# A chain of modulated convolutions on one core: 18 products for W, shared products of R between them, S's sums on VectorE

## The chip, the cores and the metric

The kernel runs on one core of a Trainium2 chip. TensorE (PE in the profile; PEld is its weight load) multiplies matrices into PSUM; VectorE (DVE), ScalarE (ACT) and GpSimd (POOL) work on tiles, and SyncE (SP) issues most DMAs. Each engine takes its own queue in order; semaphores tie the queues together. The metric is the device time of one execution in microseconds.

## The reference, cut to what matters

Four convolution layers of 64 channels and three taps (`same`, `upsample`, `same`, `downsample`) with weights that each of the 128 samples scales for itself, and the input added at the end:

```python
def _layer(x, style, w, b, mw, mb, typ):
    s = style @ mw.T + mb
    weight = SCALE * w * s[:, None, :, None]
    demod = lax.rsqrt(jnp.sum(weight * weight, axis=(2, 3)) + EPS)
    weight = weight * demod[:, :, None, None]
    if typ == 'same':
        out = jax.vmap(_conv_same)(x, weight) + b[None, :, None]
    elif typ == 'upsample':
        out = jax.vmap(_conv_up)(x, weight.transpose(0, 2, 1, 3)) + b[None, :, None]
        out = _blur(out, 2.0 * blur_k, (1, 1))
    elif typ == 'downsample':
        xb = _blur(x, blur_k, (2, 2))
        out = jax.vmap(_conv_down)(xb, weight) + b[None, :, None]
    return out
...
out = x
for i, typ in enumerate(TYPES):
    out = _layer(out, style, weights[i], biases[i], mod_w[i], mod_b[i], typ)
x = x + out
```

`x` is 128 x 64 x 1024 in float32. There is no nonlinearity between the layers.

## The kernel before, in words

Since everything is linear, the kernel folds the four layers of a sample into one filter of nine taps and applies that filter to the input once. Four samples make a quad; there are 32 quads (`NQ`), and the main loop's turn q (`turn_of`, q = 4 to 28; `early_turn` for 0 to 3, a written-out tail after 28) works on several quads at once: on q and n = q + 1 (applying the filter), on c = q + 2 (making W, the filter), and on s = q + 4 (the start of the chain of weights). The order in which each engine gets its instructions is the order in which the calls stand in the code (`manual_schedule`).

The chain of weights of one quad, each step products on TensorE in blocks of 64 columns (one block a tap) and an eviction by ScalarE that scales by the sample:

- `scale3` scales the last layer's taps (tile wd).
- `stage1_a` and `stage1_b` multiply by layer 2's taps into psS. ScalarE evicts four blocks to S (L360) behind stage1_a; behind stage1_b VectorE adds two more to them (L442), and GpSimd adds a third pair of blocks (L445).
- `stage2` multiplies S by the taps E of layer 1 with its blur, into psR. Three of its products are the same for two blocks each: `share` makes them a turn earlier from two sums of S's blocks (`share_sums`, VectorE, L462), in free columns (from NB + 4 on) of the two PSUM banks psA of quad q; `share_copy` (ScalarE, L490) copies each twice into psR, and `stage2_rest` adds the rest. ScalarE evicts to R.
- `stage3_b` and `stage3_a` multiply R by layer 0's taps to the nine taps W of the filter (L571), 12 and 7 products of 64 columns. GpSimd prepares two sums of R's blocks (`r_sums`, L588). stage3_b uses psA of quad n, four of its blocks are copied into psW by ScalarE, and stage3_a adds to those. ScalarE evicts all to Wf.
- `combine_a` and `combine_b` (VectorE) make from W the factors H of a fast form of the filter, and `residual` (L659) adds the input's share, a scaled identity, to the middle tap.

The filter is applied as five products of 340 columns (L753, `conv0` to `conv4`, each 12 matmuls in three groups) to transformed inputs T, which VectorE (`in_g01`, `in_g2`, `in04`, `in3`, L711) and GpSimd (`in1`, L726, `in2`, L731) make from the input X. psA of a quad collects conv3 (copied away by `copy_m3`), then conv1 (`sum1` on VectorE makes y1 from it), then conv2; `sum2` then makes Y from the copy and psA in two instructions, one a bank, and subtracts psA from y1 (L812); conv4 adds to Y in PSUM, conv0 to psA. `outputs(q, i)` evicts one of the three phases (psA, y1, Y) by ScalarE (L830) into the tile o and has SyncE store it.

So a turn has this order on TensorE: stage2(c), conv2(q), stage3_b(c), conv4(q), stage3_a(c), conv3(n), stage1_a(s), conv0(q), stage1_b(s), share(c + 1), conv1(n). In turns 10, 14, 15 and 19 (`SLOTS`) products for the signal's ends stand ahead of conv1. share runs in turns 5 to 27.

Of the kernel before, what the change touches and what calls it, by code (L numbers as in the profile page):

```python
# [54 lines left out]
C = 64  # L55
# [8 lines left out]
def kernel(  # L64
# [199 lines left out]
    def var_newton(bs, ls=slice(0, NL)):  # L264
# [5 lines left out]
    tA, tB, tBn, tC, t0, t3, td, tb = (  # L270
        const.tile([P, NQ, 2], F32, name=n) for n in ("tA", "tB", "tBn", "tC", "t0", "t3", "td", "tb")
# [94 lines left out]
    w2n = const.tile([P, 5, C], F32, name="w2n")  # L366

    def split_weights():
        nc_g.tensor_copy(w3x[:, :K], w3)
        nc_g.tensor_scalar_mul(w2n[:, :K], woi[2], -1.0)  # L370
        for t, src in ((w3x, w3), (w2n, woi[2])):
            nc_g.tensor_add(t[:, K:], src[:, : K - 1], src[:, 1:])
# [32 lines left out]
    EVEN = slice(0, K, 2)  # L405

    def stage1(q, pool=None, engs=(nc_a, nc_a), between=None):
# [3 lines left out]
        for k, (at, at1) in enumerate(((0, 3), (3, 1), (1, 4))):  # L411
            tap_matmul(ps, wd, at, 2, woi[2][:, k, :], EVEN, first=k == 0)
            tap_matmul(ps, wd, at1, 1, woi[2][:, k, :], slice(1, 2), last=k == K - 1)
# [3 lines left out]
        for r in range(2):  # L417
            scaled_copy(engs[r], flat(st[r][:, 1:6]), ps[r][:, : 5 * C], tB[:, q, r : r + 1])
# [3 lines left out]
    def stage1_a(q, ps=None):  # L422

        ps = ps or unit(ps_w, f"psS{q}")
        wd = chain[q]
        tap_matmul(ps, wd, 2, 2, w2n[:, 0, :], EVEN, first=True)
        tap_matmul(ps, wd, 3, 2, w2n[:, 2, :], EVEN)
        tap_matmul(ps, wd, 1, 1, w2n[:, 1, :], slice(1, 2))
        st, t = s_tiles(q)
        for r in range(2):  # L430
            scaled_copy(nc_a, flat(st[r][:, :4]), ps[r][:, C : 5 * C], tBn[:, q, r : r + 1])
        chain[q] = wd, ps, st, t

    def stage1_b(q):

        wd, ps, st, t = chain[q]
        tap_matmul(ps, wd, 2, 1, w2n[:, 3, :], slice(3, 4))
        tap_matmul(ps, wd, 4, 1, w2n[:, 4, :], slice(4, 5), last=True)
        for r in range(2):
            p1 = st[r][:, 0:1, :].to_broadcast([P, 2, C])  # L440
            sums = ps[r][:, 2 * C : 6 * C].rearrange("c (a b o) -> c a b o", a=2, b=2)[:, :, 0]
            nc_v.scalar_tensor_tensor(  # L442
                st[r][:, 4:6, :], sums, tB[:, q, r : r + 1], p1, op0=ALU.mult, op1=ALU.subtract
            )
        nc_g.tensor_add(t[:, :, 2], t[:, :, 2], t[:, :, 0])  # L445
# [7 lines left out]
    def tap_differences():  # L453
# [4 lines left out]
        nc_g.tensor_sub(Ed[:, 4:], E[:, 3:8:4], E[:, 5:6].to_broadcast([P, 2, C]))  # L458

    def share_sums(q):  # L460
        t = whole[q]
        nc_v.tensor_add(t[:, :, 6:8], t[:, :, 1:5:3], t[:, :, 2:6:3])  # L462
# [13 lines left out]
    def share(q, ps):  # L476
# [3 lines left out]
        chain_matmul(p12, E[:, 2], chain[q], slice(6, 7))  # L480
        chain_matmul(p34, E[:, 6], chain[q], slice(6, 7))
        chain_matmul(p34, E[:, 5], chain[q], slice(7, 8), True)
        shared_ps[q] = [b[:, at[0] : at[2]] for b in ps]

    def share_copy(q):

        ps = unit(ps_w, f"psR{q}")
        for r in range(2):
            src = shared_ps[q][r].rearrange("c (a o) -> c a o", a=2)
            nc_a.copy(  # L490
                ps[r][:, C : 5 * C].rearrange("c (a b o) -> c a b o", a=2, b=2),
# [4 lines left out]
    def stage2_rest(q):  # L496

        ps = shared_ps.pop(q)
        block = lambda i, n=1: [b[:, i * C : (i + n) * C] for b in ps]
        apart = [b[:, : 4 * C].rearrange("c (a b o) -> c a b o", a=2, b=2)[:, :, 0] for b in ps]  # L500
        plan = (
            (apart, E[:, 0], slice(1, 4, 2)),
            (block(1), Ed[:, 0], slice(2, 3)),
            (block(2), Ed[:, 1], slice(1, 2)),
            (block(3), E[:, 2], slice(3, 4)),
            (block(3), Ed[:, 2], slice(2, 3)),
            (block(4), Ed[:, 3], slice(1, 2)),
# [1129 lines left out]
```

## Time and profile before

| | |
|---|---|
| time, median of 3 runs | 480.93 us (480.69 to 480.96) |
| span of the profiled execution | 478.0 us |
| the profiled execution with what lies around its span, taken as in the runs | 480.9 us |
| TensorE's granted clock, mean | 0.997 |
| sum2's instructions (L662, Y from m and psA) | 64, 517 ns each |
| the first sum of W in combine and others of 384 elements (L662) | 0.55 to 0.57 us each |
| scaled copies psW from psA (L360) | 100, 269 ns each |
| evictions Wf from psW, 128 x 256 | 50, 470 ns each |
| R's sums on GpSimd (L588) | 24, 737 ns each |
| S's sums on GpSimd (L445) | 28, 790 ns each |

The span is the time from the first to the last instruction of one profiled execution; the run's time is longer by what lies around it, 2.9 us. An engine's busy time counts overlapping instructions once. A row of a timeline holds the start, the duration from the first start to the last end, engine, line, operation, output and inputs, shape and count; what stands in brackets is the engine's idle time ahead and what ended it. A product of TensorE appears as two records for each of its four quarters of the array, so eight records are one product.

### The profile page before, as it was taken

How to read it: one execution, taken by the hardware profiler on the slowest of the kernel's cores; microseconds unless marked ns; L12 is line 12 of the kernel's file. 1: busy time of each engine (PE TensorE's matmuls, PEld its weight loads, DVE VectorE, ACT ScalarE, POOL GpSimd, SP SyncE). 2: the span in 40 equal slices, each digit the busy share in tenths (PEclk: the TensorE clock that was granted, in tenths of full speed). 3: DMA queues.
4: the chain of work that ended last, by engine and by line, in shares of the span. 5: the costliest groups of instructions: out<-in, count | busy, mean ns of one | idle time of the engine just before them, and what ended most of it. 6: DMA issues, size and time to landing. Idle time of an engine off the chain costs nothing.

```text
span 478.0 us, 26721 instructions
## 1 busy us (share of the span) xinstructions
PE 469.6 (98%) x11928; PEld 346.4 (72%) x11928; DVE 417.5 (87%) x690; ACT 310.1 (65%) x708; POOL 163.5 (34%) x197
## 2 busy tenths in 40 slices
PE   8999999999999999999999999999999999999995
PEld 7877788777878876677776677766887777766652
DVE  5889998879889998899979899979989999999895
ACT  5565666667666676666667666667666768766352
POOL 3434032663335342243432233422434432333200
PEclk9999999999999999999999999999999999999998
DMA  5406365544445554345543455533455554445125
GB/s 175 158 28 200 114 195 192 150 139 144 139 150 157 173 173 127 122 151 160 171 149 120 131 170 152 173 127 126 145 169 162 162 154 146 152 146 170 61 91 191
DMA packets 50514, 70.70 MB, mean 148 GB/s; under 512 B 5664, under 2 KB 47328, under 8 KB 50400
## 3 DMA queue, kind: packets, MB, share of 16 engines
q1 hardware_dynamic: 49808, 68.32, 45.8%
q8 instruction: 93, 1.52, 1.5%
q10 hardware_dynamic: 592, 0.69, 0.5%
q14 instruction: 21, 0.17, 0.1%
HBM read 35.36 MB, written 33.62 MB: 144 GB/s over the span
## 4 chain that ended last, share of the span: by engine, by line
PE 95%; DVE 4%; issue 0%; ACT 0%; ACTq 0%; DVEq 0%
PE psA L753 45%; PE Y L753 11%; PE psR L467 9%; PE psA L571 7%; PE psW L571 7%; PE psS L389 6%; PE psR L533 4%; PE psA L467 2%; PE Y L994 2%; DVE H L662 1%; PE Y L180 1%; PE Y L336 1%; DVE G L662 0%; PE psM L204 0%; DVE o L832 0%
## 5 line engine op out<-in xcount | busy, mean ns | idle before, releaser
L753 PE MATMUL psA<-T,H 64*64 64x340 f32 x2304 | 187.3, 447 | 0.8 <-DVE y L662 0.7
L753 PEld LDWEIGHTS psA<-T,H 64*64 64x64 f32 x2304 | 89.9, 133 | 50.0 <-issue 3.1
L662 DVE SCALAR_TENSOR_TENSOR G<-X 128x1376 f32<-128x1376 f32 (+2 forms) x65 | 78.1, 1207 | 1.1 <-DMA X<-in_x 0.9
L726 POOL TENSOR_TENSOR T<-G 128x684 f32<-128x684 f32 x28 | 46.5, 1659 | 73.1 <-DVE G L662 73.1
L445 POOL TENSOR_TENSOR S<-S 128x128 f32<-128x128 f32 x28 | 22.1, 790 | 144.1 <-ACT S L360 136.8
L360 ACT ACTIVATE R<-psR,tC 128x448 f32<-128x448 f32 x63 | 36.5, 630 | 46.3 <-PE psR L467 26.7
L753 PE MATMUL psA<-T,Wf 64*64 64x340 f32 x768 | 63.9, 446 | 0.0
L753 PE MATMUL Y<-T,Wf 64*64 64x340 f32 x768 | 62.8, 451 | 0.1
L662 DVE SCALAR_TENSOR_TENSOR Y<-m,psA 128x340 f32<-128x340 f32 x64 | 33.1, 517 | 28.0 <-PE psA L753 26.6
L360 ACT ACTIVATE psW<-psA 128x128 f32<-128x128 f32 x100 | 19.3, 269 | 50.3 <-PE psA L571 46.2
L740 DVE TENSOR_TENSOR T<-G 128x1368 f32<-128x1368 f32 (+1 forms) x33 | 50.7, 1540 | 0.0
L360 ACT ACTIVATE Wf<-psW,t 128x256 f32<-128x256 f32 (+2 forms) x76 | 32.7, 479 | 26.5 <-PE psW L571 26.2
L711 DVE TENSOR_TENSOR T<-X 128x684 f32<-128x684 f32 x32 | 47.9, 1496 | 0.0
L467 PE MATMUL psR<-S,E 64*64 64x64 f32 (+1 forms) x1472 | 46.5, 238 | 0.0
L731 POOL TENSOR_TENSOR T<-G 128x684 f32<-128x684 f32 x28 | 46.5, 1660 | 0.0
L389 PEld LDWEIGHTS psS<-wd,w2n 64*64 64x64 f32 x1120 | 35.0, 133 | 13.3 <-ACT S L360 0.8
L467 PEld LDWEIGHTS psR<-S,E 64*64 64x64 f32 x1472 | 39.6, 134 | 5.2 <-ACT psR L490 0.2
L753 PEld LDWEIGHTS Y<-T,Wf 64*64 64x64 f32 x768 | 29.6, 132 | 18.0 <-DVE Y L662 0.7
L830 ACT ACTIVATE o<-psA,tb,td 128x340 f32<-128x340 f32 x63 | 37.0, 647 | 6.3 <-PE psA L753 6.3
L753 PEld LDWEIGHTS psA<-T,Wf 64*64 64x64 f32 x768 | 29.1, 133 | 15.1
L830 ACT ACTIVATE o<-Y,tb,td 128x340 f32<-128x340 f32 x63 | 36.6, 637 | 4.5 <-PE Y L753 2.7
L830 ACT ACTIVATE o<-y,tb,td 128x340 f32<-128x340 f32 x62 | 38.5, 679 | 0.6 <-DVE y L812 0.6
(165 smaller groups left out, 832.4 us busy)
## 6 DMA issues: line engine op xcount, KB each, us to landing
out<-o SPq DMA_DIRECT2D x167, 170.0 KB, 2.6
X<-in_x SPq DMA_DIRECT2D x150, 172.0 KB, 3.6
X<-in_x SPq DMA_DIRECT2D x14, 516.0 KB, 5.3
out<-o SPq DMA_DIRECT2D x6, 510.0 KB, 5.4
out<-o SPq DMA_DIRECT2D x2, 340.0 KB, 3.0
Xe<-in_x_ends SPq DMA_DIRECT2D x1, 512.0 KB, 6.7
out<-o ACTq DMA_DIRECT2D x3, 170.0 KB, 2.3
par<-in_params SPq DMA_DIRECT2D x2, 192.0 KB, 3.4
```

The lines of the kernel that those rows point to most:

```text
L360: nc_a.activation(dst, src, AF.Copy, scale=f)
L389: nc.tensor.matmul(ps[r][cols, at * C : (at + n) * C], weight[rows], wd[c if r == 0 else 1 - c][rows, taps], start=first, stop=last, skip_ ...
L445: nc_g.tensor_add(t[:, :, 2], t[:, :, 2], t[:, :, 0])
L467: nc.tensor.matmul(dst[r][cols], weight[rows], st[c if r == 0 else 1 - c][rows, slots, :], start=False, stop=last, skip_group_check=True,)
L571: nc.tensor.matmul(dst[r][cols], weight[rows], t[rows, c, slots, :], start=first, stop=last, skip_group_check=True,)
L662: nc_v.scalar_tensor_tensor(out, x, f, y, op0=ALU.mult, op1=op)
L711: nc_v.tensor_sub(t[:, pairs, 0, :NJ], plane(X, 3, pairs), plane(X, 1, pairs))
L726: eng.tensor_add(t[:, :, 0, :NJ], plane(g, 2), plane(g, 1))
L731: eng.tensor_sub(t[:, :, 1, :NJ], plane(g, 2), plane(g, 1))
L740: nc_v.tensor_sub(t[:, pairs, :, :NJ], both(a, PL), both(b, 1))
L753: nc.tensor.matmul(ps[s][cols, :NB], w, Ts[q, tag][rows, c, i, g : g + NB], start=(g == 0 and m == 3), stop=(g == K - 1), skip_group_check ...
L830: nc_a.activation(dst, src, AF.Identity, bias=add, scale=d3)
```

## The change

It regroups the products of W, moves three steps to other places in the turn, and hands two steps to other engines:

- stage3_b makes three sums' products from GpSimd's sums, now three blocks in two instructions, one a half of R; copies of three blocks go to six of psW. stage3_b and stage3_a hold 7 and 11 products of 64 columns. The six evictions of stage3_a scale by three tables (t0, t0b, t0c) instead of taps that are scaled ahead.
- S's signs change (w2n, tBn go, En comes), and its blocks lie in other slots. In the main loop VectorE makes the third sum of stage1_b; GpSimd's addition stays in the early turns.
- The residual's scaled identity x3 is made by ScalarE (`identity`) behind R's eviction; VectorE adds it in one instruction.
- sum2's two instructions become one where `wide` holds (the main loop but its first turn).
- share stands inside stage3_b, ahead of its last entry; share_sums at the end of the turn before; conv0's first group ahead of stage1_a; the outputs of Y behind S's eviction, those of y1 behind share_copy.

```diff
-    def stage1_b(q):
+    def stage1_b(q, eng=nc_v):
...
         for r in range(2):
-            p1 = st[r][:, 0:1, :].to_broadcast([P, 2, C])
-            sums = ps[r][:, 2 * C : 6 * C].rearrange("c (a b o) -> c a b o", a=2, b=2)[:, :, 0]
+            at = slice(3, 6, 1 if eng is nc_v else 2)
+            sums = blocks(ps, at)[r]
+            n = sums.shape[1]
+            p1 = st[r][:, 0:1, :].to_broadcast([P, n, C])
             nc_v.scalar_tensor_tensor(
-                st[r][:, 4:6, :], sums, tB[:, q, r : r + 1], p1, op0=ALU.mult, op1=ALU.subtract
+                st[r][:, at, :], sums, tB[:, q, r : r + 1], p1, op0=ALU.mult, op1=ALU.add
             )
-        nc_g.tensor_add(t[:, :, 2], t[:, :, 2], t[:, :, 0])
+        if eng is not nc_v:
+            eng.tensor_add(t[:, :, 4], t[:, :, 4], t[:, :, 0])
...
     def r_sums(q, eng):
         t = chain[q]
-        eng.tensor_add(t[:, :, 7:9], t[:, :, 2:6:3], t[:, :, 3:7:3])
+        for r in (slice(0, 2),) if eng is nc_v else PAIR:
+            eng.tensor_add(t[:, r, 7:10], t[:, r, 0:6:2], t[:, r, 1:7:2])
...
-    def stage3_b(q, ps):
+    def stage3_b(q, ps, between=None):
...
         plan = (
-            (slice(0, 3), w0s[2][:, 2, :], slice(0, 7, 3)),
-            (slice(0, 2), w0s[2][:, 1, :], slice(1, 5, 3)),
-            (slice(0, 2), w0s[2][:, 0, :], slice(2, 6, 3)),
-            (slice(3, 4), w0s[0][:, 0, :], slice(0, 1)),
-            (slice(4, 5), w0s[1][:, 0, :], slice(1, 2)),
-            (slice(4, 5), w0s[1][:, 1, :], slice(0, 1)),
-            (slice(5, 7), w0s[0][:, 1, :], slice(7, 9)),
+            (slice(3, 4), w0s[1][:, 2, :], slice(5, 6)),
+            (slice(3, 4), w0s[1][:, 1, :], slice(6, 7)),
+            (slice(4, 5), w0s[2][:, 2, :], slice(6, 7)),
+            (slice(0, 3), woi[0][:, 1, :], slice(7, 10)),
         )
         for i, (at, weight, slots) in enumerate(plan):
+            if between and i == len(plan) - 1:
+                between()
             same_row(blocks(ps, at), weight, t, slots, i == 0, i == len(plan) - 1)
         pw = shared_w[q] = unit(ps_w, f"psW{q}")
-        src = blocks(ps, slice(5, 7))
-        for i, f in enumerate((1.0, 1.0 / 3.0)):
-            for dst, v in zip(blocks(pw, slice(i, i + 3, 2)), src):
-                scaled_copy(nc_a, dst, v, f)
-        stage3_out(q, ps, 0, 5)
+        same_row(blocks(pw, slice(0, 1)), woi[0][:, 0, :], t, slice(0, 1))
+        for r in range(2):
+            src = ps[r][:, : K * C].rearrange("c (a o) -> c a o", o=C)
+            dst = pw[r][:, C : 7 * C].rearrange("c (a b o) -> c a b o", b=2, o=C)
+            nc_a.copy(dst, src[:, :, None, :].to_broadcast([P, K, 2, C]))
+        for r, src in enumerate(blocks(ps, slice(3, 5))):
+            scaled_copy(nc_a, Wq[q][0][:, 7:9, r], src, t0[:, q, r : r + 1])
...
     def stage3_a(q):
...
         plan = (
-            (slice(0, 3, 2), Wd[:, 0], slice(3, 7, 3)),
-            (slice(0, 3, 2), w0s[0][:, 2, :], slice(1, 5, 3)),
-            (slice(1, 4, 2), Wd[:, 1], slice(2, 6, 3)),
-            (slice(1, 2), w0s[1][:, 0, :], slice(4, 5)),
+            (slice(1, 6, 2), Wd[:, 0], slice(1, 6, 2)),
+            (slice(2, 7, 2), Wd[:, 1], slice(0, 5, 2)),
+            (slice(2, 7, 2), woi[0][:, 0, :], slice(2, 7, 2)),
+            (slice(3, 6, 2), woi[0][:, 2, :], slice(1, 4, 2)),
         )
...
-    def sum2(q, steps=(0, 1)):
+    def sum2(q, steps=(0, 1), wide=True):
         if 0 in steps:
             m3 = m3c.pop(q)
-            for s, a in enumerate(banks(q)):
-                sum_of(Y[:, s, :NB], m3[:, s], 3.0, a[:, :NB])
+            whole = parts(q) if wide else [(s, a[:, :NB]) for s, a in enumerate(banks(q))]
+            for s, a in whole:
+                sum_of(Y[:, s, :NB], m3[:, s], 3.0, a)
...
     def turn_of(q):
...
-        stage3_b(c, open_a(n))
+        stage3_b(c, open_a(n), (lambda: share(c + 1, banks(q))) if sharing(q) else None)
...
         conv3(n)
+        copy_m3(n)
         if entry:
-            copy_m3(n)
-        outputs(q, 2)
+            outputs(q, 2)
+        else:
+            conv0(q, 0)
         if s < NQ:
             stage1_a(s)
         if not entry:
-            copy_m3(n)
+            outputs(q, 2)
         in04(n)
-        if sharing(q):
-            share_sums(c + 1)
...
-        conv0(q, *((2,) if entry else range(K)))
+        conv0(q, *((2,) if entry else (1, 2)))
...
         if sharing(q):
-            share(c + 1, banks(q))
             share_copy(c + 1)
+        if not entry:
+            outputs(q, 1)
         outputs(q, 0)
...
         sum1(n)
+        if sharing(q + 1):
+            share_sums(s)
         in3(c)
```

On TensorE, the end of stage1_b, share (L467, psA from S) and the start of conv1 stood so before (lines of the kernel before; a number behind a name is the buffer's):

```order
L389 MATMUL psS_0_5072<-wd_1_4895,w2n 64x64
L389 MATMUL psS_1_5073<-wd_1_4895,w2n 64x64
L389 MATMUL psS_1_5073<-wd_0_4893,w2n 64x64
L467 MATMUL psA_4692<-S_4799,E 64x64 [waits DVE_49]
L467 MATMUL psA_4692<-S_4799,E 64x64 x11
L753 MATMUL psA_4979<-T_17_4891,H_4694 64x340 [waits Activation_49]
```

Now, with the lines of the changed kernel, the end of conv2 (L781) and stage3_b (L582) with share (L477) in it, up to the first product in psW:

```order
L781 MATMUL psA_4865<-T_17_4775,H_4586 64x340 x11
L582 MATMUL psA_5129<-R_5101,w0s_155 64x64 [waits Activation_49] x2
L582 MATMUL psA_5129<-R_5101,w0s_155 64x64 x6
L582 MATMUL psA_5129<-R_5101,w0s_156 64x64 x4
L477 MATMUL psA_4865<-S_4978,E 64x64 [waits DVE_49]
L477 MATMUL psA_4865<-S_4978,E 64x64 x7
L477 MATMUL psA_4865<-S_4978,En 64x64 x4
L582 MATMUL psA_5129<-R_5101,par 64x192 [waits Pool_49] x2
L582 MATMUL psA_5129<-R_5101,par 64x192 x2
L582 MATMUL psW_0_5160<-R_5101,par 64x64 [waits PE_49]
```

share moved from behind stage1_b to behind three products of stage3_b, into the banks that conv2 has just ended in. Its wait on VectorE (DVE_49) is for a count: before, that of share_sums; now, that of the subtraction y1 -= psA of the same turn. VectorE's queue around it, now:

```order
L690 SCALAR_TENSOR_TENSOR y_17_5034<-psA_4865,m_17_4958 128x680
L472 TENSOR_TENSOR S_4978<-S_4978 128x2x2x64
L739 TENSOR_TENSOR T_17_5037<-X_107 128x2x342
L690 SCALAR_TENSOR_TENSOR Y<-m_17_4958,psA_4865 128x2x340
L841 TENSOR_TENSOR y_17_5034<-y_17_5034,psA_4865 128x680
```

These are sum1, share_sums, in3, sum2 in one instruction, and the subtraction. share_sums stood two instructions ahead of stage1_b's sums before and now stands between sum1 and in3. On ScalarE, from the copy of conv3 or S's eviction to R's eviction, before:

```order
L830 ACTIVATE o_4780<-Y,tb,td 128x340 x2
L360 ACTIVATE S_4799<-psS_0_4785,tBn 128x256
L360 ACTIVATE S_4799<-psS_1_4786,tBn 128x256
L792 COPY m_16_4802<-psA_4692 128x680
L830 ACTIVATE o_4780<-y_15_4600,tb,td 128x340 x2
L490 COPY psR_0_4853<-psA_4409 128x256
L490 COPY psR_1_4854<-psA_4409 128x256
L830 ACTIVATE o_4780<-psA_4409,tb,td 128x340 x2
L360 ACTIVATE wd_0_4893<-w3x,tA 128x320
L360 ACTIVATE wd_1_4895<-w3x,tA 128x320
L360 ACTIVATE R_4953<-psR_0_4853,tC 128x448
```

and now:

```order
L820 COPY m_17_4958<-psA_4865 128x680
L361 ACTIVATE S_4978<-psS_0_4964,tB 128x4x64
L361 ACTIVATE S_4978<-psS_1_4965,tB 128x4x64
L859 ACTIVATE o_4981<-Y,tb,td 128x340 x2
L500 COPY psR_0_5010<-psA_4584 128x256
L500 COPY psR_1_5011<-psA_4584 128x256
L859 ACTIVATE o_4981<-y_16_4770,tb,td 128x340 x2
L859 ACTIVATE o_4981<-psA_4584,tb,td 128x340 x2
L361 ACTIVATE wd_0_5041<-w3x,tA 128x320
L361 ACTIVATE wd_1_5043<-w3x,tA 128x320
L361 ACTIVATE R_5101<-psR_0_5010,tC 128x448
L361 ACTIVATE R_5101<-psR_1_5011,tC 128x448
```

The outputs of Y and of y1 came in between S's eviction and R's; the copy m went out of it.

More of the change, by code (lines that the diff above doesn't have):

```diff
@@ L410, in stage1 @@
         ps = unit(pool or ps_w, f"psS{q}")
-        for k, (at, at1) in enumerate(((0, 3), (3, 1), (1, 4))):
-            tap_matmul(ps, wd, at, 2, woi[2][:, k, :], EVEN, first=k == 0)
-            tap_matmul(ps, wd, at1, 1, woi[2][:, k, :], slice(1, 2), last=k == K - 1)
+        plain.add(q)
+        for k in range(K):
+            tap_matmul(ps, wd, k, K, woi[2][:, k, :], slice(0, K), first=k == 0, last=k == K - 1)
         if between:
@@ L650, in stage3, with identity, residual @@
                 )
-        stage3_out(q, ps, *((3, 6), (0, 3))[part], engs)
+        stage3_out(q, ps, kinds, engs)
         return ps
-    def residual(q):
+    def identity(q):
+        for r in range(2):
+            nc_a.activation(x3[:, r], idn3, AF.Copy, scale=t3[:, q, r : r + 1])
+    def residual(q, made):
         W = Wq[q][0]
+        if made:
+            v = W[:, tap(1, 1)]
+            nc_v.tensor_add(v, v, x3)
+            return
         for r in range(2):
@@ L673, in combine_a @@
         sum_of(h1, c, -2.0, a)
-        residual(q)
+        residual(q, made)
         sum_of(h3, h1, 1.0 / 6.0, b)
@@ L1462, in turn_of @@
         if sharing(q):
-            share(c + 1, banks(q))
             share_copy(c + 1)
+        if not entry:
+            outputs(q, 1)
         outputs(q, 0)
@@ L1494 @@
     stage3(c, 0)
-    sum2(q, (0,))
+    sum2(q, (0,), False)
     combine_a(n)
@@ L1515 @@
     conv2(n)
-    sum2(n, (0,))
+    sum2(n, (0,), False)
     combine_b(c, (1,))
@@ L1540 @@
     conv0(q, 1, 2)
-    sum2(n)
+    sum2(n, wide=False)
     for i in range(2):
```

138 lines of the change are left out of this document (76 added, 62 removed).

## The prediction, made before the changed kernel was run

> **What bounds the kernel now.** I read the page first, for busy shares and for the chain that ended last.
>
> ```profile
> PE 469.6 (98%) x11928; PEld 346.4 (72%) x11928; DVE 417.5 (87%) x690; ACT 310.1 (65%) x708; POOL 163.5 (34%) x197
> ...
> PE 95%; DVE 4%; issue 0%; ACT 0%; ACTq 0%; DVEq 0%
> PE psA L753 45%; PE Y L753 11%; PE psR L467 9%; PE psA L571 7%; PE psW L571 7%; PE psS L389 6%; PE psR L533 4%; PE psA L467 2%; PE Y L994 2%; DVE H L662 1%; PE Y L180 1%; PE Y L336 1%; DVE G L662 0%; PE psM L204 0%; DVE o L832 0%
> ```
>
> TensorE (PE) is busy for 98% of the 478.0 us span and holds 95% of the chain. Whatever takes products from it gains, as long as no other engine makes it wait. Next come two turns by the window view, and the second of them by the timeline of PE.
>
> ```profile
> 379.12:392.96 13.84, 13.84 (x388) 9.82 (x384) 12.88 (x19) 9.85 (x23) 4.83 (x5) 1.00 0.55 163
> 392.96:406.81 13.85, 13.85 (x389) 10.21 (x385) 12.86 (x19) 9.84 (x23) 4.84 (x5) 1.00 0.48 150
> ```
>
> ```profile
> 392.96 0.94 PE L571 MATMUL psA<-R,w0s 64*64 64x192 f32 x24
> 393.73 0.29 PE L571 MATMUL psA<-R,par 64*64 64x64 f32 x8
> 393.84 0.46 PE L571 MATMUL psA<-R,w0s 64*64 64x64 f32 x14
> ...
> 394.33 1.96 PE L753 MATMUL Y<-T,Wf 64*64 64x340 f32 x24
> 396.10 0.41 PE L571 MATMUL psW<-R,wsq 64*64 64x128 f32 x8
> ...
> 396.75 0.31 PE L571 MATMUL psW<-R,w0s 64*64 64x64 f32 x8
> 396.87 1.91 PE L753 MATMUL psA<-T,H 64*64 64x340 f32 x24
> 398.58 0.74 PE L389 MATMUL psS<-wd,w2n 64*64 64x128 f32 x24
> ...
> 400.85 0.42 PE L389 MATMUL psS<-wd,w2n 64*64 64x64 f32 x16
> 401.08 0.54 PE L467 MATMUL psA<-S,E 64*64 64x64 f32 x24
> 401.43 1.91 PE L753 MATMUL psA<-T,H 64*64 64x340 f32 x24
> 403.15 0.41 PE L467 MATMUL psR<-S,E 64*64 64x128 f32 x8
> ```
>
> A turn is 13.85 us and PE is busy for all of it: every other engine's work is hidden. Durations in a row overlap the next row, so I price by distances between starts. A product of 340 columns in three groups takes 1.72 (401.43 to 403.15), that is 0.573 a group and 0.108 for 64 columns. A 64-column product in fact takes 0.115 (393.73 to 393.84; 400.85 to 401.08 for two), a 128-column one 0.217 (396.10 to 396.75 for three).
>
> **PE's work.** stage3_b and stage3_a held four 64-column products, six of 128 and one of 192; they now hold four, one and four. Five times 0.217 go and three times 0.323 (three times 0.108) come: **-0.12 us a turn**, in 25 turns (q = 4 to 28). stage2 and stage1_a/b keep their products; stage1 in the prologue packs the same columns into half as many, below 0.1 us in all.
>
> **The moved shared products.** This is the step that decides. share's three products stood behind stage1_b, at 401.08. Now they stand inside stage3_b, behind its first three 64-column products, 0.345 (3 x 0.115) after conv2 ends. The order of the built program gives the first of them a wait on VectorE, and the count waited for is that of the subtraction y1 -= psA: it reads the two banks that share writes, and stands ahead of share in the program. VectorE reaches it so:
>
> ```profile
> 387.73 0.60 DVE L442 SCALAR_TENSOR_TENSOR S<-psS,tB,S 128x128 f32<-128x128 f32 x2
> 388.24 1.58 DVE L662 SCALAR_TENSOR_TENSOR G<-X 128x1376 f32<-128x1376 f32 x1
> 389.74 0.86 DVE L662 SCALAR_TENSOR_TENSOR y<-psA,m 128x680 f32<-128x680 f32 x1
> 390.52 1.87 DVE L711 TENSOR_TENSOR T<-X 128x684 f32<-128x684 f32 x1
> 393.21 1.07 DVE L662 SCALAR_TENSOR_TENSOR Y<-m,psA 128x340 f32<-128x340 f32 x2 [0.82 <-PE psA L753]
> 394.19 0.85 DVE L812 TENSOR_TENSOR y<-y,psA 128x680 f32<-128x680 f32 x1
> ```
>
> Call 392.96, where stage3_b starts, zero. sum2's pair starts at 0.25, since VectorE has waited 0.82 for conv2 itself; the subtraction starts at 1.23 and ends at 2.08. With the pair as one instruction of 2 x 340 the nearest row is 389.74, the same size from the same banks, 0.86. Starts follow each other about 0.09 before the end, so the subtraction starts at 1.02 and ends at 1.88. If the merging saved nothing it would still be 2.08: those are the two ends, and I take 1.89, by the row of equal size.
>
> What a release costs shows at conv4: the pair ended at 394.28 (393.21 + 1.07) and conv4 started at 394.33, 0.05 later, then needed 1.77 to 396.10 where 1.72 is usual: another 0.05. So share runs as if from 1.99, where PE was ready at 0.345: **a stall of 1.64**. Nothing can fill it: PE takes its queue in order, and behind share stand the rest of stage3_b, conv4 and stage3_a, then conv3, which are ready by then or soon after. In return conv4's own 0.09 (stage3_b's products sum to 1.32, but it started after 1.37, and 0.05 more) goes, since sum2 has ended by 1.11. Net in a turn with share: 1.64 - 0.09 - 0.12 = **+1.43**; q = 5 to 27 are 23 such turns: **+32.9**.
>
> The row speaks for no cost of the old place: at 401.08 share followed stage1_b with no gap, as nothing read its banks then. The Trainium skill ("PSUM — Partial Sum Buffer", section "PSUM bank collisions raise a hardware error") asks for guarding PSUM by bank and quadrant, not by address. By that rule the columns behind NB that share writes are no protection against the read of the first 340, and the sum is the one above; by addresses alone share would wait for nothing here and the sum would be the first rival's. No run here shows a collision.
>
> **What the stall covers.** Two other engines get tighter; alone each would cost something.
>
> ```profile
> 385.51 0.84 ACT L360 ACTIVATE S<-psS,tBn 128x256 f32<-128x256 f32 x2 [0.32 <-PE psS L389]
> 386.24 0.72 ACT L792 COPY m<-psA 128x680 f32<-128x680 f32 x1
> 386.84 1.25 ACT L830 ACTIVATE o<-y,tb,td 128x340 f32<-128x340 f32 x2
> 388.15 0.63 ACT L490 COPY psR<-psA 128x256 f32<-128x256 f32 x2
> 388.68 1.18 ACT L830 ACTIVATE o<-psA,tb,td 128x340 f32<-128x340 f32 x2
> 389.74 1.02 ACT L360 ACTIVATE wd<-w3x,tA 128x320 f32<-128x320 f32 x2
> 391.54 1.16 ACT L360 ACTIVATE R<-psR,tC 128x448 f32<-128x448 f32 x2 [0.78 <-PE psR L467]
> ```
>
> ScalarE first. From S's eviction to R's it had 6.03 us (385.51 to 391.54). conv0's first group (0.573) and share (0.345) leave that window, so 5.11 stay. In it now stand S 0.73, the outputs of Y 1.06 (as those of psA, 388.68 to 389.74), share's copies 0.53, the outputs of y 1.15, of psA 1.06 and wd 0.92: 5.45, with some 0.1 of waiting for VectorE. R would be 0.3 to 0.5 late, and stage3_b's start 0.2 to 0.3.
>
> ```profile
> 389.99 1.67 POOL L726 TENSOR_TENSOR T<-G 128x684 f32<-128x684 f32 x1 [2.73 <-DVE G L662]
> 392.78 0.73 POOL L588 TENSOR_TENSOR R<-R 128x256 f32<-128x256 f32 x1 [1.12 <-ACT R L360]
> ...
> 247.23 0.86 DVE L711 TENSOR_TENSOR T<-X 128x684 f32<-128x684 f32 x1
> ```
>
> GpSimd second. in3 takes VectorE 0.86 alone but 1.87 beside in1 on GpSimd: it ended 0.73 after in1 did (391.66), so it stood still meanwhile. share_sums now stands ahead of in3 behind the same in1 and ends about 0.3 after it; stage1_b also ends 0.34 nearer the turn's end, as share is no longer behind it. So in3 ends near zero instead of 0.57 before it, and the two sums of R (192 elements each, about 0.6 by the 0.73 of 256) end near 1.0 instead of 0.55. stage3_b's last entry would want them at 0.69. Both delays end before 1.99, so **neither is paid** in the 23 turns. In q = 28, which has no share, R's lateness and sum2 cost about 0.5, less 0.2 saved; q = 4 gains 0.12.
>
> The remaining edits cost nothing here. ScalarE's two identities and six evictions of W for two add some 0.8 us to 9.84 of 13.85; W's last eviction has all of conv3 and conv0's first group to land before stage1_a. VectorE's third block of S (0.60 for two pieces of 128, some 0.13 more) has the new 1.4 us. The residual becomes one instruction. The outputs' stores move with them on SP's queue; the tile they leave is wanted two turns later.
>
> **The sum.** 32.9 + 0.3 (q = 28) - 0.1 (q = 4) = +33.1. The profiled execution spans 478.0, and the runs' median is 480.93, so 2.9 lie around the span and are kept: 480.93 + 33.1 = **514.0**.
>
> **The rivals.**
> - *Only the late R and the late sums are paid* (share's wait ends early, or doesn't bind). They overlap, so the later one counts: sums ready near 1.0, 0.05 to release and 0.05 to restart, against 0.69: 0.41 - 0.09 - 0.12 = +0.20 in some 19 turns. Those with matmuls of the ends are spared:
>
> ```profile
> 248.35 1.16 ACT L360 ACTIVATE R<-psR,tC 128x448 f32<-128x448 f32 x2 [2.65 <-PE psR L467]
> ```
>
>   There ScalarE had 2.65 to spare, so q = 10, 14, 15 and 19 pass it on to no one. 19 x 0.20 - 6 x 0.12, and 0.3 for q = 28: +3.4, about **484**. The rows give no reason why share should not wait; chance 0.03.
> - *PE's products alone decide*: VectorE, ScalarE and GpSimd all arrive before PE wants them, place stage3_b. 25 x 0.12 = 3.0, about **478**, faster. It decides if the subtraction ends before 0.29 behind conv2, where sum2 alone starts at 0.25; chance 0.02.
> - *The wait is longer*: in3 ends later still and holds sum2 on VectorE, 0.3 a turn if R's first sum on GpSimd goes ahead of in3 (0.6 less what in3 has already had). 23 x 0.3 = 6.9, **521**. For it speaks the 1.87 of in3; against it, that R now comes late, so in3 is first. Chance 0.10.
> - *The forecast*, 514: chance 0.85. Its own ends: subtraction at 2.08 rather than 1.89 gives 23 x 0.19 = +4.4; no restart cost and PE's other waits covered by the new one, 23 x 0.05 and 1 to 2 us, give -3.
>
> **Range and chances.** 510 to 520 takes in the bounds of the forecast and leaves out the first two rivals (0.05), the third (0.10) and some of the edges. A measurement here can tell about 0.2% (1 us) from no change. Faster 0.02 (the second rival), within 0.2% 0.01 (a third of the first, whose low end lies there), slower 0.97.
>
> **What would show it.** In the changed profile a pure turn should take 15.2 to 15.4 instead of 13.85; PE should stand still some 1.6 us inside stage3_b, ended by VectorE's y subtraction; sum2 should be one instruction of about 0.87; and the step from conv4 to the next turn's conv2 should hold no new wait. A turn of 14.0 with two small gaps (at R and at GpSimd's sums) would mean the first rival; share starting before the subtraction ends would prove the reading of its wait wrong.

## The result, and the profile after

The changed kernel takes **519.82 us** (median of 4 runs, 518.73 to 520.63) against 480.81 us for the kernel before beside it: a ratio of 1.0821 (95% interval 1.0796 to 1.0846), 39.0 us more. The prediction said 514.0, within 510 to 520; applied to its 480.93, the ratio gives 520.4, just above that range. The profiled execution, the longest of the four runs, spans 518.8 us instead of 478.0.

The page of the changed kernel, busy time first and the chain that ended last behind it:

```profile
PE 477.2 (92%) x11432; PEld 342.9 (66%) x11432; DVE 421.6 (81%) x642; ACT 340.0 (66%) x806; POOL 157.8 (30%) x198
...
PE 65%; DVE 11%; ACT 2%; issue 1%; POOL 0%; ACTq 0%; DVEq 0%; POOLq 0%
```

These shares are of the whole span, and the view follows this chain back to 97 us only, over 418 of the 518.8 us, while before it followed nearly all of the span. Of what it follows, TensorE went from 95% to 81% (65% x 518.8 / 418) and VectorE from 4% to 14%. Who waits for whom, by the view of waits (us in total, times, longest), with the group of share's first matmuls from the page:

```profile
PEld psA L477 <- DVE y L841: 33.0, 23, 2.3
PE psA L477 <- DVE y L841: 29.8, 23, 2.1
...
L477 PE MATMUL psA<-S,E 64*64 64x64 f32 x368 | 10.6, 230 | 29.8 <-DVE y L841 29.8
```

23 turns have a share, and in all 23 it waits for VectorE's subtraction (y, now L841), 1.3 us of idle matmuls and 1.4 of idle weight loads each. Here is such a turn in the timeline (start, duration, engine, line, tile); stage3_b starts at 428.54:

```profile
427.59 1.15 ACT L361 ACTIVATE R<-psR,tC 128x448 f32<-128x448 f32 x2
...
427.74 0.86 DVE L739 TENSOR_TENSOR T<-X 128x684 f32<-128x684 f32 x1
428.29 1.31 POOL L604 TENSOR_TENSOR R<-R 128x192 f32<-128x192 f32 x2 [0.76 <-ACT R L361]
428.54 0.83 PE L582 MATMUL psA<-R,w0s 64*64 64x64 f32 x24
...
428.86 0.87 DVE L690 SCALAR_TENSOR_TENSOR Y<-m,psA 128x680 f32<-128x680 f32 x1 [0.25 <-PE psA L781]
...
429.63 0.86 DVE L841 TENSOR_TENSOR y<-y,psA 128x680 f32<-128x680 f32 x1
...
430.55 0.46 PE L477 MATMUL psA<-S,E 64*64 64x64 f32 x16 [1.18 <-DVE y L841]
430.83 0.30 PE L477 MATMUL psA<-S,En 64*64 64x64 f32 x8
430.94 0.51 PE L582 MATMUL psA<-R,par 64*64 64x192 f32 x8
```

sum2 is one instruction of 0.87, the subtraction ends at 430.49 (429.63 + 0.86, 1.95 behind the start), and share follows 0.06 later. R ends 0.20 behind the start (428.74) and its sums 1.06 (429.60); both lie inside the wait. By the window view, turns q = 5, 6, 7, 14 and a pure one (26), before and then after (start:end, length, then the busy time and instructions of PE, PEld, DVE, ACT and POOL, PE's granted clock, DMA share, GB/s); the pure turn of before is the prediction's 13.84:

```profile
105.69:120.03 14.34, 14.34 (x394) 11.13 (x390) 12.25 (x21) 9.77 (x23) 6.53 (x9) 1.00 0.54 161
120.03:134.74 14.71, 14.18 (x392) 11.99 (x388) 12.57 (x21) 9.77 (x23) 6.40 (x18) 1.00 0.49 147
134.74:148.63 13.89, 13.89 (x388) 9.85 (x384) 12.63 (x20) 9.78 (x23) 6.30 (x7) 1.00 0.49 152
234.20:249.76 15.56, 15.56 (x412) 11.35 (x408) 12.32 (x21) 9.77 (x23) 5.17 (x5) 1.00 0.51 157
```

```profile
106.50:123.87 17.37, 14.41 (x378) 11.29 (x374) 13.40 (x20) 10.93 (x28) 6.88 (x9) 1.00 0.40 123
123.87:140.97 17.10, 14.25 (x377) 11.07 (x373) 12.26 (x19) 11.11 (x29) 6.31 (x18) 1.00 0.40 122
140.97:157.06 16.09, 14.42 (x372) 9.92 (x365) 12.25 (x18) 10.36 (x27) 4.41 (x6) 1.00 0.36 116
251.32:271.04 19.72, 17.57 (x397) 11.71 (x395) 13.08 (x21) 11.57 (x30) 5.24 (x6) 0.91 0.42 121
443.88:459.22 15.34, 14.16 (x372) 9.94 (x368) 13.12 (x18) 11.00 (x28) 4.58 (x5) 1.00 0.44 135
```

Where the 40.8 us of the span are, from such rows of all turns:

| part | after less before | predicted |
|---|---|---|
| 23 turns with a share, 15.34 - 13.84 = 1.50 each | +34.5 | +32.9 |
| q = 5, 6, 7 above that (3.03 + 2.39 + 2.20 - 3 x 1.50) | +3.1 | 0 |
| q = 14 above that (4.16 - 1.50) | +2.7 | 0 |
| from q = 28 on | +0.7 | +0.3 |
| up to q = 4 | +0.9 | 0 |
| the other turns, q = 4 among them | -1.1 | -0.1 |

In the other turns the growth lies between 0.5 less than 1.50 (q = 11) and 0.4 more (q = 12); these were not taken apart. The part up to stage3_b of q = 4 is scatter: it took 92.3 to 96.3 us in the profiled executions of nine kernels with the same code there. So the mechanism is the one forecast, 0.07 a turn larger, and some 6 us lie in four turns that the prediction had passed over.

### The profile page after: what moved, and what is told of

Same layout as the page of the kernel before. It is cut to its first block, busy times and chain, and to the rows that moved or that the text cites. A ratio compares the mean times of both kernels' runs of the same rounds, so it can differ in the third digit from the quotient of the medians.

```text
span 518.8 us, 25798 instructions
## 1 busy us (share of the span) xinstructions
PE 477.2 (92%) x11432; PEld 342.9 (66%) x11432; DVE 421.6 (81%) x642; ACT 340.0 (66%) x806; POOL 157.8 (30%) x198
## 4 chain that ended last, share of the span: by engine, by line
PE 65%; DVE 11%; ACT 2%; issue 1%; POOL 0%; ACTq 0%; DVEq 0%; POOLq 0%
PE psA L781 32%; PE Y L781 9%; PE psR L477 8%; PE psW L582 7%; DVE Y L690 4%; DVE y L841 4%; PE psS L394 3%; PE psA L477 3%; PE psA L582 2%; PE Y L1024 2%; ACT o L859 1%; DVE G L690 1%; DVE S L472 1%; PE psR L544 0%; DVE y L690 0%
## 5 line engine op out<-in xcount | busy, mean ns | idle before, releaser
L781 PE MATMUL psA<-T,H 64*64 64x340 f32 x2304 | 186.5, 447 | 0.9 <-DVE y L690 0.6
L781 PEld LDWEIGHTS psA<-T,H 64*64 64x64 f32 x2304 | 87.7, 133 | 50.8 <-issue 2.8
L781 PE MATMUL psA<-T,Wf 64*64 64x340 f32 x768 | 67.7, 446 | 0.0
L781 PE MATMUL Y<-T,Wf 64*64 64x340 f32 x768 | 62.7, 455 | 0.1
L627 ACT COPY psW<-psA 128x384 f32<-128x384 f32 x50 | 21.2, 467 | 63.2 <-PE psW L582 58.5
L361 ACT ACTIVATE Wf<-psW,t 128x192 f32<-128x192 f32 (+1 forms) x76 | 30.1, 446 | 44.2 <-PE psW L582 43.3
L451 DVE SCALAR_TENSOR_TENSOR S<-psS,tB,S 128x192 f32<-128x192 f32 (+1 forms) x56 | 20.1, 400 | 41.9 <-PE psS L394 40.9
L690 DVE SCALAR_TENSOR_TENSOR H<-Wf 128x384 f32<-128x384 f32 x64 | 46.1, 720 | 0.0
L690 DVE SCALAR_TENSOR_TENSOR Y<-m,psA 128x680 f32<-128x680 f32 (+1 forms) x40 | 29.1, 729 | 15.4 <-PE psA L781 14.3
L781 PEld LDWEIGHTS Y<-T,Wf 64*64 64x64 f32 x768 | 28.6, 135 | 17.6 <-issue 0.9
L604 POOL TENSOR_TENSOR R<-R 128x192 f32<-128x192 f32 x48 | 31.1, 669 | 23.8 <-ACT R L361 23.8
L781 PEld LDWEIGHTS psA<-T,Wf 64*64 64x64 f32 x768 | 27.6, 133 | 16.2
L477 PE MATMUL psA<-S,E 64*64 64x64 f32 x368 | 10.6, 230 | 29.8 <-DVE y L841 29.8
L361 ACT ACTIVATE S<-psS,tB 128x256 f32<-128x256 f32 (+1 forms) x63 | 26.9, 477 | 16.6 <-PE psS L394 16.6
```

Source lines behind the costliest of these rows:

```text
L361: nc_a.activation(dst, src, AF.Copy, scale=f)
L477: nc.tensor.matmul(dst[r][cols], weight[rows], st[c if r == 0 else 1 - c][rows, slots, :], start=False, stop=last, skip_group_check=True,)
L604: eng.tensor_add(t[:, r, 7:10], t[:, r, 0:6:2], t[:, r, 1:7:2])
L627: nc_a.copy(dst, src[:, :, None, :].to_broadcast([P, K, 2, C]))
L690: nc_v.scalar_tensor_tensor(out, x, f, y, op0=ALU.mult, op1=op)
L781: nc.tensor.matmul(ps[s][cols, :NB], w, Ts[q, tag][rows, c, i, g : g + NB], start=(g == 0 and m == 3), stop=(g == K - 1), skip_group_check ...
```

## The experiments

Each is the changed kernel or the kernel before with the edit shown. Times are medians beside runs of the kernel before on the same chip; turns come from the profiled execution.

### What share waits for

**e1_share_back.** Share stands behind stage1_b again, all else stays.

```diff
-        stage3_b(c, open_a(n), (lambda: share(c + 1, banks(q))) if sharing(q) else None)
+        stage3_b(c, open_a(n))
...
         if sharing(q):
+            share(c + 1, banks(q))
             share_copy(c + 1)
```

> The changed kernel with one thing undone: share's three products stand behind stage1_b again, just ahead of share_copy; all else stays. Theory (PE stands still at share because the subtraction y1 -= psA still reads the banks that share writes): the wait at share goes, and what stays is R's late start and late sums (about 0.45 a turn at stage3_b's last entry, less 0.21 for conv4's wait and the lighter products, so about +0.24 a turn) and the moved outputs of Y in the turns q = 5 to 7 (about +3): 484 to 491, a pure turn near 14.1. Rival (the 39 us lie in the late R, the moved sums and the other edits, and share only shows them): above 510.

Measured: 490.81 us, ratio 1.0238 (1.0185 to 1.029). 29 of the 39 us are gone with one moved call. The turn is 14.14, and PE has no idle time in it by the window view; its waits show as matmuls that take longer than their columns ask, and as waiting weight loads:

```profile
405.69:419.83 14.14, 14.14 (x373) 10.54 (x372) 12.87 (x17) 10.93 (x29) 4.58 (x5) 1.00 0.48 151
```

```profile
405.69 0.53 PE L582 MATMUL psA<-R,w0s 64*64 64x64 f32 x24
...
406.00 0.87 DVE L690 SCALAR_TENSOR_TENSOR Y<-m,psA 128x680 f32<-128x680 f32 x1 [0.59 <-ACT x L676]
406.04 0.81 PE L582 MATMUL psA<-R,par 64*64 64x192 f32 x5
...
406.46 0.14 PEld L582 LDWEIGHTS psA<-R,par 64*64 64x64 f32 x3 [0.29 <-POOL R L604]
...
406.93 1.38 PE L781 MATMUL Y<-T,Wf 64*64 64x340 f32 x16
```

The last entry of stage3_b begins at 406.04 with the matmuls whose half of R's sums is there; the others wait until GpSimd ends its second sum at 406.40. Yet this wait is not what the turn pays. conv4 starts 0.06 behind the end of sum2 (406.87), 1.24 behind stage3_b's start, where the products ahead of it are worth 0.78 (three of 0.115, 0.323, 0.115). In e1's turn q = 28 GpSimd's sums end 0.43 behind the start instead of 0.71, and conv4 starts at 1.24 all the same. The 0.30 over the kernel before is conv4's start (1.24 instead of 1.37) and a longer stage3_a, 1.19 instead of 0.77. (The view puts sum2's wait down to ScalarE's identity; in g1_no_identity below, which has none, sum2 starts no earlier.)

**e2_share_behind_conv4.** Share's call stands between conv4 and stage3_a.

```diff
             combine_a(n, True)
             conv4(q)
+            if sharing(q):
+                share(c + 1, banks(q))
```

> The changed kernel with share's products behind conv4 and ahead of stage3_a, 2 us later than in the change and still ahead of conv0 and stage1_b. Theory (only the subtraction's end counts): conv4 runs while the subtraction does, share follows without a wait, so 484 to 495, above the kernel with share at its old place only by what ScalarE's and VectorE's tighter windows ask. Rival (any place ahead of conv0's products makes share wait, for its sums or for another reader of psA): above 510.

Measured: 495.32 us, ratio 1.0316 (1.028 to 1.0353), a turn of 14.42 with no wait at share. So an early place is possible; it is the 1.6 us before the subtraction's end that cost. Why this turn is 0.28 longer than e1's was not taken apart.

**e3_share_alone.** The kernel before, with share moved into stage3_b and share_sums to the end of the turn, nothing else.

```diff
-        stage3_b(c, open_a(n))
+        stage3_b(c, open_a(n), (lambda: share(c + 1, banks(q))) if sharing(q) else None)
...
-        if sharing(q):
-            share_sums(c + 1)
...
-            share(c + 1, banks(q))
             share_copy(c + 1)
...
         sum1(n)
+        if sharing(q + 1):
+            share_sums(s)
         in3(c)
```

> The kernel before, with nothing but share moved to its new place (inside stage3_b, ahead of its last entry) and share_sums to the end of the turn before. Theory: six entries of stage3_b stand ahead of share here, so PE comes to it at about 1.1 after conv2's end; sum2 is still two instructions, so the subtraction ends at 2.08: a stall of about 1.0 less conv4's 0.09 in 23 turns, +23 with some more for late sums: 499 to 510. Rival (the place of share is harmless; what costs is the new arithmetic of R and W and the wide sum2): 480 to 483.

Measured: 503.33 us, ratio 1.0503 (1.0448 to 1.0558); 23 x (14.82 - 13.84) = 22.5. With 12 products in stage3_b, more of them stand ahead of share, so the same wait is shorter:

```profile
427.33 1.07 DVE L664 SCALAR_TENSOR_TENSOR Y<-m,psA 128x340 f32<-128x340 f32 x2 [0.33 <-PE psA L755]
...
428.31 0.85 DVE L814 TENSOR_TENSOR y<-y,psA 128x680 f32<-128x680 f32 x1
...
429.22 0.58 PE L467 MATMUL psA<-S,E 64*64 64x64 f32 x24 [0.84 <-DVE y L814]
```

**f1_sub_behind.** The changed kernel with the subtraction behind share in the program, so that share waits for sum2 alone.

```diff
-            sum2(q)
+            sum2(q, (0,))
...
         stage3_b(c, open_a(n), (lambda: share(c + 1, banks(q))) if sharing(q) else None)
+        if not entry:
+            sum2(q, (1,))
```

> The changed kernel with the subtraction y1 -= psA behind share's products in the program instead of ahead of them, so that share waits on sum2 alone, which reads the same two banks. Theory (share waits for the last reader of its banks that stands ahead of it): share starts about 0.78 earlier (0.85 for the subtraction, less the overlap of starts), the turn goes from 15.34 to 14.5 to 14.65, 500 to 504 in all, as long as the later subtraction holds nobody. Rival (share waits for something else that comes as late, its sums or a read of S): no change, 518 or more.

Measured: 500.61 us, ratio 1.0431 (1.0406 to 1.0456), a turn of 14.58, 0.76 less than 15.34.

```profile
410.98 0.87 DVE L690 SCALAR_TENSOR_TENSOR Y<-m,psA 128x680 f32<-128x680 f32 x1 [0.26 <-PE psA L781]
...
411.90 0.46 PE L477 MATMUL psA<-S,E 64*64 64x64 f32 x16 [0.42 <-DVE Y L690]
412.19 0.30 PE L477 MATMUL psA<-S,En 64*64 64x64 f32 x8
...
412.55 0.86 DVE L841 TENSOR_TENSOR y<-y,psA 128x680 f32<-128x680 f32 x1 [0.70 <-PE psA L477]
```

Share now starts 0.05 behind sum2's end, and the subtraction waits for share. The four runs together leave one reading: share waits for the last read of its two banks that the program puts ahead of it, wherever share stands. In f1 that read is sum2's, of the first 340 columns alone, and share writes behind them; whether the wait is kept by bank or by tile no run here tells.

### The turns beyond the wait

**e4_outputs_back.** ScalarE's outputs of Y stand ahead of copy_m3 and S's eviction again.

```diff
+        outputs(q, 2)
         copy_m3(n)
-        if entry:
-            outputs(q, 2)
-        else:
+        if not entry:
             conv0(q, 0)
         if s < NQ:
             stage1_a(s)
-        if not entry:
-            outputs(q, 2)
```

> The changed kernel with one thing undone: ScalarE's outputs of Y stand ahead of copy_m3 and of S's eviction again. Theory (in the turns q = 5, 6 and 7 VectorE's read of Y's high columns, the memset and so the small matmul and S's sums wait for the late outputs): these turns take 15.9, 16.2 and 15.4 instead of 17.37, 17.09 and 16.09, a pure turn stays at 15.34 (S is later on ScalarE, but the share's stall covers it), 516 to 518 in all. Rival (those turns are longer for the share's wait or late sums): they stay, 519 to 521.

Measured: 527.0 us, ratio 1.0975 (1.0955 to 1.0995): **slower** than the change, half a miss. Turns 5, 6, 7 and a pure one:

```profile
106.54:122.77 16.23, 14.67 (x378) 10.52 (x371) 13.84 (x20) 10.38 (x27) 6.62 (x8) 1.00 0.37 117
122.77:138.67 15.90, 14.61 (x376) 10.45 (x372) 13.15 (x19) 10.85 (x29) 6.46 (x18) 1.00 0.43 135
138.67:154.40 15.73, 14.44 (x372) 10.84 (x368) 12.96 (x18) 10.68 (x28) 5.03 (x7) 1.00 0.44 138
433.80:449.60 15.80, 14.60 (x373) 10.92 (x368) 13.24 (x18) 10.84 (x28) 4.57 (x5) 1.00 0.46 137
```

Less their kernel's pure turn, the first three took 0.50, 0.87 and 0.05 before, 2.03, 1.76 and 0.75 after, and 0.43, 0.10 and -0.07 here: the extra went with the edit. The changed kernel's timeline of the turn q = 5 shows why, VectorE first and one row of TensorE behind it:

```profile
117.49 0.26 DVE L960 TENSOR_TENSOR cc<-Y,a 128x96 f32<-128x96 f32 x1 [2.77 <-ACT o L859]
117.78 0.26 DVE L961 SCALAR_TENSOR_TENSOR cc<-b1s,cc 128x96 f32<-128x96 f32 x1
118.06 0.14 DVE L1486 MEMSET Y<- 128x96 f32 x1
118.10 0.66 DVE L451 SCALAR_TENSOR_TENSOR S<-psS,tB,S 128x192 f32<-128x192 f32 x2
...
118.34 0.30 PE L1269 MATMUL Y<-cc,wsum 64*64 64x96 f32 x2 [1.44 <-DVE Y L1486]
```

VectorE reads Y's columns behind 340 (L960) only when ScalarE's late outputs of Y's first 340 are done, though both only read, and S's sums stand behind it in the queue. A small product of TensorE (L1269) waits 1.44 for the memset behind it, here and in q = 6. But the pure turn grew by 0.46, which I had put at nothing. ScalarE's S now ends at 444.00 (443.09 + 0.91) in a turn where stage1_b's weights wait for it:

```profile
443.69 0.19 PEld L394 LDWEIGHTS psS<-wd,w2n 64*64 64x64 f32 x4 [0.56 <-ACT S L361]
444.05 0.25 PEld L394 LDWEIGHTS psS<-wd,w2n 64*64 64x64 f32 x10 [0.17 <-ACT S L361]
```

That is a second wait of PE at another place of the turn, behind share, so the one at share cannot cover it.

**e5_late_early.** VectorE's second half of g (side work of q = 13) stands beside the first half.

```diff
-        13: lambda: setup1(0),
+        13: lambda: (setup1(0), setup1(1)),
...
-    LATE = {13: lambda: setup1(1)}
+    LATE = {}
```

> The changed kernel with one piece of q = 13's side work (VectorE's second half of g, 1.41 long behind in3) put beside the first half, where VectorE waited 1.63 for PE. Theory (in3 ends 0.6 later than before the change, so this piece now holds sum2, and with it the subtraction and share, in the turn q = 14): share's wait there goes from 2.15 to 1.18, so 1.0 to 2.5 less (the upper end if conv4's gaps in that turn come from it too): 517.3 to 518.9. Rival (q = 14 is long for other reasons): no change, 519.5 to 520.5.

Measured: 517.55 us, ratio 1.0779 (1.076 to 1.0797). The turn q = 14 is 17.07 instead of 19.72, which is 15.56 + 1.51: all of its extra is gone. In the change, g's second half (251.29 to 252.70) stood between in3 and sum2, and share waited 2.15. The rest of the extra was PE's clock. The window view of that turn in the changed kernel, cut into pieces:

```profile
251.32:253.50 2.18, 0.83 (x28) 0.57 (x23) 2.15 (x5) 0.67 (x3) 2.18 (x3) 1.00 0.86 207
253.50:256.00 2.50, 1.71 (x52) 1.26 (x56) 2.44 (x5) 0.60 (x2) 0.68 (x1) 0.89 0.70 207
256.00:258.00 2.00, 2.00 (x20) 1.02 (x16) 1.96 (x3) 0.79 (x3) 0.00 (x0) 0.50 0.34 116
258.00:260.00 2.00, 2.00 (x40) 1.53 (x36) 1.52 (x2) 0.00 (x0) 0.00 (x0) 0.78 0.00 0
```

The granted clock fell to 0.50: the lost parts of the pieces (0.11 x 2.50 + 0.50 x 2.00 + 0.22 x 2.00) add up to 1.7 us. It fell in e4 too (0.92 over the turn), not in g1_no_identity, whose turn q = 14 took 18.03 with the same wait: 1.0 us is g's, 1.7 the clock's. The expectation's "conv4's gaps" were the clock.

**g1_no_identity.** ScalarE's two identities and the residual in one instruction are undone.

```diff
-        if not entry:
-            identity(n)
...
-            combine_a(n, True)
+            combine_a(n)
```

> The changed kernel with the scaled identity and the wide residual undone: VectorE adds the identity itself in two instructions, ScalarE has two instructions less behind R's eviction. Theory (these two edits are hidden, in the turns with the share's wait and elsewhere): a pure turn stays at 15.34 and the time within 1 us of 519.8. Rival (sum2 starts 0.07 later than before behind conv2 because ScalarE's identities run there): sum2 starts 0.25 instead of 0.32 behind stage3_b's start, a turn of 15.27, 518.

Measured, in one run: 518.74 us, a pure turn of 15.34; the time lies inside the change's own 518.73 to 520.63. The edits are hidden. sum2 still starts 0.32 behind stage3_b's start, so the identities are not why it starts 0.07 later than before.

### The products without the moves

**c0_products.** The 18 products, tables and instructions of the change, every order of the kernel before.

```diff
-        stage3_b(c, open_a(n), (lambda: share(c + 1, banks(q))) if sharing(q) else None)
+        stage3_b(c, open_a(n))
...
-        copy_m3(n)
         if entry:
-            outputs(q, 2)
-        else:
-            conv0(q, 0)
+            copy_m3(n)
+        outputs(q, 2)
...
+        if sharing(q):
+            share_sums(c + 1)
...
-        conv0(q, *((2,) if entry else (1, 2)))
+        conv0(q, *((2,) if entry else range(K)))
...
         if sharing(q):
+            share(c + 1, banks(q))
             share_copy(c + 1)
-        if not entry:
-            outputs(q, 1)
```

> The new products, tables and instructions of the change with every order of the kernel before: share and share_sums, outputs, conv0 and conv1 at their old places. Theory: no wait at share, R is in time, but three products (0.345) stand ahead of the entry that needs R's sums, which end near 0.6 on GpSimd: a stall of about 0.3, less conv4's 0.09 and PE's 0.12: a pure turn of 13.9 to 14.0, 481.5 to 485. Rival (the new arithmetic alone saves its 0.12 and 0.09): 475.5 to 478.

Measured: 493.75 us, ratio 1.0281 (1.0265 to 1.0298), a turn of 14.46: a miss by half a microsecond a turn. Two rows of the view of waits say what I had left out:

```profile
PEld psS L394 <- ACT Wf L361: 12.8, 24, 0.6
PEld Y L781 <- DVE Y L690: 5.4, 22, 0.7
```

By the timeline conv4 starts 1.31 behind stage3_b's start (1.37 before), although only 0.78 of products are left ahead of it: it waits for sum2. Behind conv4, stage3_a has grown from 0.77 to 1.19. The products were not taken from PE's busy time but moved from ahead of conv4, where they covered sum2, to behind it. And stage1_a's weights wait for W's last evictions, of which there are now six: conv3 to stage1_a takes 1.83 instead of 1.71. These three (-0.06, +0.42, +0.12) make 0.48 of the turn's 0.62; the rest lies between stage1_a and the next stage3_b and isn't taken apart.

**c1_vector_sums.** c0_products with R's sums on VectorE, ahead of sum2, and psW's first product ahead of the entry that needs them.

```diff
-            r_sums(c, nc_g)
+            r_sums(c, nc_v)
...
+            if i == len(plan) - 1:
+                pw = shared_w[q] = unit(ps_w, f"psW{q}")
+                same_row(blocks(pw, slice(0, 1)), woi[0][:, 0, :], t, slice(0, 1))
```

> The same as c0_products, but R's two sums stand on VectorE ahead of sum2, where it waits for conv2's end anyway, and psW's first product goes ahead of the entry that needs them. Theory: R ends 0.2 ahead of conv2's end, the sums 0.3 behind it, and the entry wants them at 0.46: no stall, so a pure turn of 13.63 to 13.75, 475.5 to 478.5. Rival (R ends later, or the sums push sum2 and conv4 back by what they take): 480 or more.

Measured: 512.62 us, ratio 1.0676 (1.0655 to 1.0697), a turn of 15.38: a clear miss.

```profile
402.11 2.28 POOL L758 TENSOR_TENSOR T<-G 128x684 f32<-128x684 f32 x1
...
403.26 1.54 DVE L604 TENSOR_TENSOR R<-R 128x384 f32<-128x384 f32 x1 [0.38 <-ACT R L361]
...
404.73 0.86 DVE L689 SCALAR_TENSOR_TENSOR Y<-m,psA 128x680 f32<-128x680 f32 x1
```

The sum ended only 0.41 behind in2 on GpSimd (404.80 and 404.39), and sum2 started 0.9 later than in c0. Without GpSimd beside it the sum is short: 0.55 to 0.56 in the turns q = 11, 14, 15, 16 and 20 of this run, where no GpSimd work overlaps it, and 0.56 to 0.59 in the turn q = 4, where VectorE makes it in all the kernels with the new products. In q = 11, 15 and 20 sum2 then starts 0.38 behind stage3_b's start, as in c0. While r_sums stood on GpSimd, ahead of in2, it kept in2 out of this place; moved away, it met it. The Trainium skill ("SBUF — State Buffer", section "SBUF: two separate sides") describes the port that the two engines share as an exclusive lock for an instruction with two SBUF inputs; the trace agrees, with 1.54 beside 0.56 and the end just behind in2's.

### One edit of the change alone

**b1_wide** and **b2_wide** are one kernel, the one before with sum2 as one instruction in the main loop, timed 10 and 12 times.

```diff
-            for s, a in enumerate(banks(q)):
-                sum_of(Y[:, s, :NB], m3[:, s], 3.0, a[:, :NB])
+            whole = parts(q) if wide else [(s, a[:, :NB]) for s, a in enumerate(banks(q))]
+            for s, a in whole:
+                sum_of(Y[:, s, :NB], m3[:, s], 3.0, a)
```

> The kernel before, with nothing but sum2's two 340-column instructions made one of 2 x 340. Theory: conv4's wait of 0.09 goes in 25 turns, so 478 to 479.5. Rival (conv4's 0.09 is not a wait for sum2, or the wide one takes as long as the pair): 480.5 to 481.5, no change.

> The same kernel as b1_wide, timed in more rounds, to tell whether it is faster than the kernel before. Theory: a turn of 13.75 instead of 13.84, so 0.09 x 25 = 2.2 us less, ratio 0.995. Rival (the gain of the turns is lost elsewhere): ratio 0.999 to 1.001.

Measured: 479.09 us, ratio 0.9982 (0.9959 to 1.0004), and 477.87 us against 479.69, ratio 0.9966 (0.995 to 0.9982). The turn is 13.75 in both, the 0.09 of conv4's wait less:

```profile
405.97:419.72 13.75, 13.75 (x388) 12.41 (x384) 12.79 (x18) 9.84 (x23) 4.91 (x5) 1.00 0.51 157
```

It is the one edit of the change that a run here shows to gain, and the gain is a third of a per cent or less; the first ten runs alone don't tell it from none.

## Why the prediction was right or wrong

The step that failed is "the remaining edits cost nothing here": what it put at nothing cost 3.1 us in q = 5 to 7, and the sum had no term at all for q = 14, where 2.7 us went. The mechanism that carries the sum, share's wait, came as forecast; its term was 0.07 a turn too small, 1.6 us in all.

- **Share's wait in stage3_b: right in its cause, its place and nearly its size.** The subtraction was put at 1.88 to 2.08 behind stage3_b's start and ended at 1.95; the turn grew by 1.50 where 1.43 was said. The mis-sized term is sum2's start: 0.32 behind the start, not 0.25. Counted from the start of conv2's last matmul it starts 0.58 later in the change, e1, f1 and g1, 0.51 in the kernel before and e3, and 0.49 in c0, which has the new products too. g1 rules out the identities. In the change's own turns q = 11, 15, 16 and 20 it is 0.50 to 0.52, so the new instructions alone don't make it either; what the 0.07 is stays open.
- **PE's work, -0.12 a turn: right as a count, wrong as a gain.** c0 and e1 show that products went from ahead of conv4 to behind it, and that sum2 is then uncovered. The prediction subtracted 0.12 without asking what the old products covered; at share's stall this did not show. The rival "PE's products alone", 478, was out of reach even without any move.
- **R and its sums late, covered by the stall: right.** Against stage3_b's start R ended 0.46 later than before (0.3 to 0.5 was said) and the sums at 1.06 (1.0 was said). The step also had stage3_b's start 0.2 to 0.3 late; that did not come: it stands 1.72 behind conv2's start (426.82 to 428.54), the usual length of a product. With the stall gone (e1) the turn is 14.14, near the 13.84 + 0.20 of the first rival, but not by its mechanism: sum2 holds conv4 longer than R's sums hold stage3_b, and the late sums stay hidden.
- **"The remaining edits cost nothing here": wrong in three turns, +3.1 us.** The step took the moved outputs as stores and as ScalarE's time. It missed that VectorE reads other columns of Y in q = 5 to 7 and is kept behind ScalarE's reads, with S's sums queued behind it. e4 takes the extra away. e4 also shows why the outputs cannot simply go back: S's eviction is then late for stage1_b, 0.46 a turn.
- **No term for q = 14: +2.7 us.** in3's later end was in the prediction, but the work that stands behind in3 in one turn was not looked for. e5 removes it all; in the profiled execution 1.7 of it was the lower clock behind the longer wait.
- **q = 28: +0.7 in place of +0.3, its reason wrong.** R was in time there (0.26 ahead of stage3_b, as before). conv4's start (1.24 instead of 1.37) and stage3_a (1.19 instead of 0.77) make 0.3, so that the forecast's 0.3 fits by luck; the other 0.4 was not taken apart.
- The rival of a longer wait, 521, lies near the measured time but did not happen: in3 ended 0.06 behind stage3_b's start and did not hold sum2 in a pure turn. It did in q = 5, where it ended 0.66 behind the start; in q = 14 the work behind it did.

## What to carry to other kernels

Before a product is moved ahead, list the reads of its PSUM banks that stand ahead of its new place, other columns included, and take the end of the last as its start. Before products are removed from a place, ask which wait they covered; work that is moved behind a wait is not saved. And read the exceptional turns of a loop as well as its steady one: side work that hid in a gap is what a shifted engine runs into first.

## What the runs showed of the hardware

- PE stood still for 2.15 us in the turn q = 14 of the changed kernel, and behind it the granted clock was 0.50 for some 3.4 us (twice the 1.7 lost); in e4 it fell in the same way, and in g1, whose weight loads waited as long (2.29 and 2.28), it stayed at 1.00. Waits of 1.2 to 1.5 in the other 22 turns with a share were not followed by it. The Trainium skill ("TensorE: Matmul & The Clock Gate", Part 1) gives half rate as the state of an idle array, reached after about 3.4 us of idle; the half rate agrees, the idle time here was shorter.
- The two-input sum of R took VectorE 0.55 to 0.59 alone and 1.54 beside GpSimd's in2. in2 itself took 2.28 there instead of 1.64; VectorE's in3 was still running when it started, and in q = 14, where in3 ran beside in2 but no sum of R did, in2 took 2.27.
